# Spreading the softmax's inverse sums through memory, and folding an output projection into the values' weights, in a four-layer image kernel

## The chip, the cores and the metric

The kernel runs on one core of one Trainium2 chip. The metric is the device time of one execution in microseconds; the three timed runs before the change gave 4995.19, 4997.74 and 5000.49 us, so the median is 4997.74 us. The profile is of one execution of the same program. Everything is computed in 32-bit floating point.

## The reference, cut to what matters

The input is a batch of two images of 128 channels and 64 by 64 pixels (4096 pixels). Four layers follow one another:

- layer 0: an embedding, then two state-space ("mamba") blocks with feed-forward parts, run along the 4096 pixels, and a residual
- layer 1: spatial self-attention with 3x3 convolutions for queries, keys and values, and a 1x1 output projection
- layer 2: spatial self-attention with plain projections
- layer 3: convolutions at four scales, a small attention across the scales, normalisation and a fusing projection

The change concerns layers 1 and 2:

```python
# layer 1
q, k, v = conv3x3(x, Wq, bq), conv3x3(x, Wk, bk), conv3x3(x, Wv, bv)    # each 128 x 4096
attn = softmax(einsum('bci,bcj->bij', q, k) * 128**-0.5, axis=2)       # 4096 x 4096
out  = einsum('bij,bcj->bci', attn, v)
x    = x + conv1x1(out, Wo, bo)
# layer 2
attn = softmax(einsum('nci,ncj->nij', q, k), axis=-1)                   # 4096 x 4096
x    = gamma * einsum('ncj,nij->nci', v, attn) + x
```

## The kernel before, in words

The whole program is one `tile_conv_seq`. The images stay in one buffer `xt` on the chip from the first layer to the last. The order of the instructions on each engine is written out by hand: the schedule is manual, so each engine and each issuing queue runs its instructions in the order in which the Python code records them, and waits where a buffer or a value is not ready.

**Layer 0.** Each image has 8 chunks of 512 pixels, and each chunk passes two blocks, which makes 32 items. An item has 32 slots; in each slot one scan runs on VectorE (`scan`, line 411), and the function `background(i)` hangs the other work of neighbouring items on numbered slots of item `i`: embedding, normalisation, projections, gates. Item -1 (`i == -1`) is the lead-in, in which no scan runs yet. There the first chunk goes through its whole chain, and slots 1, 7 and 8 to 10 load and prepare weights: `load_rest` (line 178) loads the 3x3 weights of layer 1 into three tiles `raw`; `fold(which)` (lines 197 to 206) turns each, ten VectorE instructions for each of queries, keys and values, into weights for a fast convolution along the width; `fold_out` (line 210), in slot 23, writes these to `ufold` in memory. Later in the same lead-in come the first `dtb` copies (line 382), the first `times_b` (line 393) and then the scans.

**Layers 1 and 2.** There are four runs: two layers times two images. A run takes its 4096 queries in 16 groups of 256, and each group has 8 units, so there are 512 units in all. A unit `now` consists of:

- `score` (line 759): for 128 queries, the scores against 1024 keys on TensorE; VectorE copies them out of the accumulators and takes maxima (line 764)
- `product` (line 809), 14 units later (`LAG`): for the group's 256 queries, four of the 32 steps of the product of the transposed exponentials `pt` with the values `vt`, into an accumulator `po`

Around them, every four units make a block of 128 queries: `exponentials` (line 774, ScalarE), and twice `turn`: VectorE transposes 32x32 blocks into `tr` (line 789, two buffers), and the blocks are then moved to their partitions in `pt` by four copies on GpSimd (line 796), four transfers issued by ScalarE (line 798) and eight issued by SyncE (line 800). `turn` also computes the inverse sums `rec` of the block, one value for each query, with the queries along the partitions.

The product has the queries along its columns, so each group must turn its 256 inverse sums from a column into a row that stands on all 128 partitions. In the kernel before that is done on the engines: `diagonals` (line 814) multiplies the identity by the inverse sums into two 128x128 tiles `dg` on VectorE, `spread` (line 820) multiplies each by a matrix of ones on TensorE into `pr`, and ScalarE copies that to `rb` (line 822). `divide` (line 834) then multiplies `po` by `rb` into `on`. In layer 1 `finish_mm` (line 841) multiplies `on` by the output projection into an accumulator, two units later, and `finish` (line 845) adds bias and residual into `xt`; in layer 2 `divide` itself adds `gamma` times the result (line 836).

Each transfer signals its end on one of eight semaphores, taken in turn by the transfers of SyncE and ScalarE together, and as built a transfer also waits for the one before it on its semaphore, which is the one eight transfers earlier.

Of the kernel before, what the change touches and what calls it, by code (L numbers as in the profile page):

```python
# [6 lines left out]
F32 = mybir.dt.float32  # L7
AF = mybir.ActivationFunctionType
ALU = mybir.AluOpType
# [6 lines left out]
P = 128  # L16
# [51 lines left out]
def tile_conv_seq(ctx: ExitStack, tc, x, consts, vecs, wemb, wlay, wconv, wdt, wqkv, wsmall, wms, out):  # L68
# [27 lines left out]
    ufold = [ud.tile([P, 18, C], F32, name=f"ufold{k}") for k in range(3)]  # L96

    dkept = [ud.tile([P, 6, 18 * 16], F32, name=f"dkept{k}") for k in range(4)]

    ident = kc[:, K_ID : K_ID + P]  # L100
    cm = kc[:, K_CM : K_CM + P]
# [2 lines left out]
    def v1(name, i=0):  # L104
        return vec[:, VEC[name] + i : VEC[name] + i + 1]
# [10 lines left out]
    with tc.manual_schedule(), ExitStack() as s:  # L116
# [8 lines left out]

        we = wp.tile([P, 2, C], F32, name="we")
        nc.sync.dma_start(we, wemb)


        sel = wp.tile([P, 32], F32, name="sel")  # L130
# [42 lines left out]
        raws, folded = [], []  # L173

        def load_rest():
            for which in range(3):
                raw = sp.tile([P, 3, 3, C], F32, name="raw", tag="h", bufs=5)
                nc.sync.dma_start(raw.rearrange("p y x c -> p (y x) c"), wqkv[:, which])
                raws.append(raw)
            for c in range(NCH):  # L180
                load_x(1, c)
# [4 lines left out]
        for c in range(2, NCH):  # L186
            load_x(0, c)
        load_layer(1)

        def fold(which):  # L190

# [301 lines left out]
        def background(i):  # L493

            todo = [[] for _ in range(NSL)]

            def at(t, f, *a):
                todo[t].append((f, a))

            n, p, q, r = i + 1, i - 1, i - 2, i + 2  # L500
            if has(q):
                at(3, gelu, q)
                at(6, ffn_down, q, (0, 1)), at(7, ffn_down, q, (2, 3)), at(9, ffn_add, q)
                at(11, out_mm, q), at(12, out_add, q)
            if has(p):
                at(7, y_out, p, 1), at(7, gate, p)
                at(9, mix_out, p), at(11, mix_add, p)
            if has(n):
                at(0, pu_taps, n, 0, (0, 1)), at(1, pu_taps, n, 0, (2, 3)), at(2, pu_out, n, 0)
                at(3, pu_taps, n, 1, (0, 1)), at(4, pu_taps, n, 1, (2, 3)), at(5, pu_out, n, 1)  # L510
                at(13, xproj, n), at(14, xproj_out, n), at(14, spread_bc, n, 0), at(22, spread_bc, n, 1)
                at(15, dtproj, n, 0), at(16, dtproj, n, 1), at(17, soft_plus, n), at(18, dt_end, n)
            if has(i):
                at(1, pz_mm, i, 0), at(3, pz_out, i, 0)
                at(5, pz_mm, i, 1), at(6, pz_out, i, 1)
            if has(i) or has(n):
                at(11, silu, i, n)
            if i == -1:
                at(1, load_rest), at(7, prepare, 1)
                for k in range(3):  # L520
                    at(8 + k, fold, k), at(23, fold_out, k)
                at(19, spread_dtu, 0), at(26, times_b, 0)
            pair = [(k, second) for k, second in ((p, True), (r, False)) if has(k)]
            if has(r):
                at(10, embed, r), at(11, embed_out, r)
            w, m = {}, len(pair)
            for k, (it, second) in enumerate(pair):
                at(12 + 2 * k, ln_centre, w, k, it)
                at(13 + 2 * k, ln_square, w, k, it)
                at(27, ln_spread, w, k, m), at(28, ln_scale, w, k, it)  # L530
                at(29, ln_shift, w, k, it, second)
            if pair:
                at(17, ln_var, w, m), at(18, ln_eps, w, m), at(19, ln_rs, w, m), at(20, ln_newton, w, m), at(21, ln_step, w, m)
            if has(p):
                for f in range(4):
                    at(30 + f // 2, ffn_up, p, f)
            if has(i):
                at(24, y_out, i, 0)
            return todo
# [56 lines left out]
            nc.scalar.activation(dst, src, AF.Identity, bias=bias)  # L596

        def bias(r, which):
            return v1("b" + "qkv"[which] + "12"[runs[r][0]])


# [206 lines left out]
                rhs = sta["pt", r, grp, jt // NTH][:, :, jt % NTH, :]  # L808
                nc.tensor.matmul(sta["po", r, grp], lhsT=sta["vt"][:, jt, :], rhs=rhs, start=(jt == 0), stop=(jt == N // P - 1))  # L809

        def diagonals(r, grp):
            for it in range(2):
                dg = sta["dg", it] = sp.tile([P, P], F32, name="dg", tag="dg", bufs=2)
                nc.vector.tensor_scalar(dg, ident, sta["rec", r, grp][:, it : it + 1], None, ALU.mult)

        def spread(r, grp):

            pr = psm.tile([P, QG], F32, name="pr", tag="m")
            for it in range(2):
                nc.tensor.matmul(pr[:, it * P : (it + 1) * P], lhsT=ones, rhs=sta["dg", it], start=True, stop=True)  # L820
            rb = sta["rb", r, grp] = sp.tile([P, QG], F32, name="rb", tag="rb", bufs=2)
            nc.scalar.copy(rb, pr)

        def xg(r, grp):
            l, b = runs[r]
            if l:
                k = QG // W
                return xt[:, b, 1 + grp * k : 1 + (grp + 1) * k, 1 : W + 1]
            cc, i = divmod(grp, 4)
            return xt[:, b, 1 + 16 * cc : 17 + 16 * cc, 1 + i : W + 1 : 4]  # L830

        def divide(r, grp):
            on = sta["on", r, grp] = sp.tile([P, QG], F32, name="on", tag="on")
            nc.vector.tensor_tensor(on, sta.pop(("po", r, grp)), sta.pop(("rb", r, grp)), ALU.mult)
            if runs[r][0]:
                nc.vector.scalar_tensor_tensor(xg(r, grp), rows(on), v1("gamma"), xg(r, grp), ALU.mult, ALU.add)

        def finish_mm(r, grp):
            if not runs[r][0]:
                sta["p2", r, grp] = psm.tile([P, QG], F32, name="p2", tag="m")  # L840
                nc.tensor.matmul(sta["p2", r, grp], lhsT=wa[:, WS_O : WS_O + C], rhs=sta["on", r, grp], start=True, stop=True)

        def finish(r, grp):
            if not runs[r][0]:
                nc.vector.scalar_tensor_tensor(xg(r, grp), sta.pop(("p2", r, grp)).rearrange("p (h w) -> p h w", w=16), v1("bo1"), xg(r, grp), ALU.add, ALU.add)

        def in_turn(f, u0):

# [51 lines left out]
        layers.close()  # L900
        sp = s.enter_context(tc.tile_pool(name="ats", bufs=1, reuse_waits="tile"))
        psa = s.enter_context(tc.tile_pool(name="atpa", bufs=2, reuse_waits="tile", space=PSUM))
        psm = s.enter_context(tc.tile_pool(name="atpm", bufs=1, reuse_waits="tile", space=PSUM))
        for now in range(NALL + LAG + 10):
            r, u = divmod(now, NU)
            w = now % 8
            if now < NALL:
# [42 lines left out]
                elif u == LAG:  # L950
                    load(0, LO), load(0, HI)
                    if r == 0:
                        load(1, LO)
            if w == 7:
                in_turn(lambda r, u: finish_mm(r, u // 8), LAG + 9)
            in_turn(product, LAG)
            if w == 7:
                in_turn(lambda r, u: finish(r, u // 8), LAG + 9)
            if w in (3, 7):
                in_turn(lambda r, u: exponentials(r, u // 4), 3)  # L960
            if w in (1, 5):
# [1 line left out]
            if w in (3, 7):  # L963
                in_turn(lambda r, u: turn(r, u // 4, 1), 7)
            if w == 2:
                in_turn(lambda r, u: diagonals(r, u // 8), 10)
            if w == 3:
                in_turn(lambda r, u: spread(r, u // 8), 11)
            if w == 5:
                in_turn(lambda r, u: divide(r, u // 8), LAG + 7)  # L970
            if now < NCC:
# [501 lines left out]
```

## Time and profile before

| | |
|---|---|
| time, median of three runs | 4997.74 us |
| profiled execution: span from first to last instruction | 4994.0 us |
| median of the runs less that span | 3.7 us |
| TensorE busy | 4661.7 us, 93% of the span |
| VectorE busy | 4022.4 us, 81% |
| ScalarE busy | 2358.4 us, 47% |
| GpSimd busy | 2335.3 us, 47% |
| transfers of `pt` issued by SyncE and by ScalarE | 2048 and 1024, of 64 KB, 2.0 and 2.2 us to landing |

The profiled execution has no separate time; its span stands 3.7 us below the median of the runs. In the profile PE is TensorE's matmul, PEld its weight load, DVE VectorE, ACT ScalarE, POOL GpSimd and SP SyncE; SPq and ACTq are transfers that these two issue. A line such as `L809 PE MATMUL po<-pt,vt` names the line of the kernel, the engine, the output and the inputs. One 32-bit matmul of the program stands as two records. Layer 0 takes the first 2060 us or so, the two attentions last until about 4218 us, and layer 3 takes the rest.

### The profile page before, as it was taken

What the parts mean: (1) busy time and instruction counts of PE and PEld (TensorE: products, weight loads), DVE (VectorE), ACT (ScalarE), POOL (GpSimd) and SP (SyncE); (2) the same over time, 40 slices, a digit from 0 to 9 for tenths busy, and PEclk for the clock granted to TensorE, in tenths of its full rate; (3) what the DMA queues carried; (4) which work ended last, traced back from release to release, by engine and by line L of the source; (5) the groups of instructions that cost most, each with busy time, mean ns of one, the idle gap of its engine ahead of it and who ended that gap; (6) DMA issues with size and microseconds to landing.
All of it is one profiled execution on the core that took longest, in us unless ns stands there. A gap on an engine that the chain in (4) does not pass through costs nothing.

```text
span 4994.0 us, 48951 instructions
## 1 busy us (share of the span) xinstructions
PE 4661.7 (93%) x14797; PEld 2242.2 (45%) x14797; DVE 4022.4 (81%) x4283; ACT 2358.4 (47%) x3218; POOL 2335.3 (47%) x1974
## 2 busy tenths in 40 slices
PE   6898899899988899899999999999999999999997
PEld 2222222222222222366667766666666666333332
DVE  7999999999999999778886677767776775667776
ACT  4677777777777777532222222233233332323332
POOL 3777777666777777513332233323333332333331
PEclk7889998998999989899999999999999999999998
DMA  6233333332333333224444344434444443000000
GB/s 165 68 69 69 69 71 73 71 69 65 67 67 69 69 70 68 71 57 110 109 109 126 105 111 113 118 97 111 113 98 98 110 114 87 3 7 7 5 7 9
DMA packets 242343, 386.24 MB, mean 77 GB/s; under 512 B 88592, under 2 KB 88992, under 8 KB 233632
## 3 DMA queue, kind: packets, MB, share of 16 engines
q1 hardware_dynamic: 192928, 315.94, 26.1%
q10 hardware_dynamic: 49152, 67.17, 5.4%
q8 instruction: 118, 1.93, 0.2%
q14 instruction: 145, 1.19, 0.1%
HBM read 101.02 MB, written 13.37 MB: 23 GB/s over the span
## 4 chain that ended last, share of the span: by engine, by line
PE 46%; POOL 24%; issue 12%; DVE 9%; DMA 3%; SPq 2%; ACT 2%; ACTq 0%; DVEq 0%; POOLq 0%
POOL h L414 19%; PE po L809 13%; PE pq L759 13%; DVE tr L789 3%; DMA pt<-tr 3%; PE pa L656 2%; PE pf L1130 2%; SPq L800 2%; PE pqkv L1157 2%; PE pw L1216 1%; POOL dtu L374 1%; POOL z L437 1%; PE pb L656 1%; PE pfus L1281 1%; PE psc L1181 1%
## 5 line engine op out<-in xcount | busy, mean ns | idle before, releaser
L796 POOL COPY pt<-tr 32x512 f32<-32x512 f32 x1024 | 648.8, 634 | 1439.2 <-DVE tr L789 704.5
L411 DVE TENSOR_TENSOR_SCAN h<-da,carry,h 128x512 f32<-128x512 f32 x1024 | 1240.7, 1265 | 62.0 <-ACT da L400 31.8
L414 POOL TENSOR_TENSOR h<-h,cb 128x2048 f32<-128x2048 f32 x256 | 1160.8, 4535 | 20.7
L759 PE MATMUL pq<-k,q 128*128 128x512 f32 x2048 | 962.6, 593 | 6.9 <-DVE sc L764 6.9
L809 PE MATMUL po<-pt,vt 128*128 128x256 f32 x4096 | 965.6, 379 | 2.5 <-DMA pt<-tr 2.5
L774 ACT ACTIVATE sc<-sc,nm 128x2048 f32<-128x2048 f32 x256 | 510.5, 1995 | 914.9 <-DVE nm L770 685.8
L809 PEld LDWEIGHTS po<-pt,vt 128*128 128x128 f32 x4096 | 777.9, 190 | 294.8 <-issue 208.3
L764 DVE TENSOR_SCALAR_CACHE_REDUCE sc<-pq 128x1024 f32<-128x1024 f32 x512 | 624.7, 1221 | 315.4 <-PE pq L759 293.8
L400 ACT ACTIVATE da<-dtb,am 128x512 f32<-128x512 f32 x1024 | 681.4, 684 | 220.9 <-DVE h L411 207.6
L789 DVE STREAM_TRANSPOSE tr<-sc 128x2048 f32<-128x2048 f32 x256 | 591.6, 2311 | 65.6 <-DMA pt<-tr 56.3
L393 DVE TENSOR_TENSOR h<-bb,pdu 128x2048 f32<-128x2048 f32 x256 | 581.3, 2271 | 77.6 <-PE py L426 29.4
L426 PE MATMUL py<-h,sel 128*32 128x512 f32 x2048 | 510.8, 642 | 1.6 <-POOL h L414 1.6
L759 PEld LDWEIGHTS pq<-k,q 128*128 128x128 f32 x2048 | 382.9, 190 | 283.0 <-issue 247.2
L387 PE MATMUL pdu<-dtu,fsel 128*128 128x512 f32 x512 | 327.6, 726 | 103.0 <-DVE h L393 100.6
L426 PEld LDWEIGHTS py<-h,sel 128*32 128x32 f32 x2048 | 115.3, 118 | 415.9 <-issue 409.0
L314 PE MATMUL pu<-xn,wu 128*128 128x512 f32 x512 | 246.4, 615 | 7.2 <-ACT u L320 5.5
L387 PEld LDWEIGHTS pdu<-dtu,fsel 128*128 128x128 f32 x512 | 96.6, 215 | 310.2 <-DVE h L393 185.9
L413 POOL COPY carry<-h 128x4 f32<-128x4 f32 x256 | 47.7, 186 | 389.8 <-DVE h L411 389.8
L1223 DVE TENSOR_TENSOR ov<-v,pw 128x2048 f32<-128x2048 f32 x64 | 146.1, 2284 | 62.1 <-PE pw L1216 62.1
L1157 PE MATMUL pqkv<-f,ws 128*128 128x512 f32 x384 | 188.1, 615 | 3.0 <-DVE prod L1174 2.3
L1227 POOL TENSOR_TENSOR ov<-ov 128x2048 f32<-128x2048 f32 x16 | 72.5, 4534 | 235.7 <-DVE ov L1223 235.7
L374 POOL TENSOR_TENSOR dtu<-dt,u 128x1024 f32<-128x1024 f32 x32 | 75.2, 2350 | 188.7 <-ACT dt L368 188.7
(259 smaller groups left out, 5262.2 us busy)
## 6 DMA issues: line engine op xcount, KB each, us to landing
pt<-tr SPq DMA_DIRECT2D x2048, 64.0 KB, 2.0
dtb<-dt SPq DMA_DIRECT2D x1024, 64.0 KB, 2.0
pt<-tr ACTq DMA_DIRECT2D x1024, 64.0 KB, 2.2
bb<-dr SPq DMA_DIRECT2D x128, 256.0 KB, 4.4
cb<-dr SPq DMA_DIRECT2D x128, 256.0 KB, 4.7
uw<-ufold SPq DMA_DIRECT2D x12, 576.0 KB, 4.9
uw<-dkept SPq DMA_DIRECT2D x20, 288.0 KB, 3.1
xt<-in_x SPq DMA_DIRECT2D x16, 256.0 KB, 4.8
```

The lines of the kernel that those rows point to most:

```text
L387: nc.tensor.matmul(pdu, lhsT=four(s_ % 4), rhs=st[i]["dtu"][:, s_ // 4, :], start=True, stop=True)
L393: nc.vector.tensor_tensor(h, st[i]["bc", 0], pdu.unsqueeze(1).to_broadcast([P, 4, CH]), ALU.mult)
L400: nc.scalar.activation(da, st[i]["dtb", s_], AF.Exp, scale=am[items[i][1]][:, j, gg, m : m + 1])
L411: nc.vector.tensor_tensor_scan(h[:, m, :], da, h[:, m, :], carries[b, l][:, j, gg, m : m + 1], ALU.mult, ALU.add)
L414: nc.gpsimd.tensor_tensor(h, h, st[i]["bc", 1], ALU.mult)
L426: nc.tensor.matmul(py[r : r + 32, :], lhsT=sel, rhs=st[i]["h", s_ + k][:, m, :], start=(m == 0), stop=(m == 3), tile_position=(0, r),)
L759: nc.tensor.matmul(pq[:, i, :], lhsT=sta["q", r, grp][:, it * P : (it + 1) * P], rhs=sta["k"][:, at : at + CH], start=True, stop=True)
L764: nc.vector.tensor_scalar(dst, pq, 1.0, None, ALU.mult, ALU.max, accum_out=sta["mx"][:, c2 : c2 + 1])
L774: nc.scalar.activation(sc, sc, AF.Exp, bias=nm, scale=scale, accum_out=sm[:, hh : hh + 1])
L789: nc.vector.transpose(tr, sta.pop(("sc", r, blk, hh)).rearrange("p (t r f) -> p r t f", r=NB, f=32))
L796: nc.gpsimd.tensor_copy(dst, src)
L809: nc.tensor.matmul(sta["po", r, grp], lhsT=sta["vt"][:, jt, :], rhs=rhs, start=(jt == 0), stop=(jt == N // P - 1))
```

## The change

The inverse sums go through memory. Two small tensors `sums`, of 2 by 128 values, are added in memory. `sums_out` writes the 256 inverse sums of a group there from `rec` (128 partitions, two values each, that stand 128 values apart in memory), and `sums_in`, two units later, reads the 256 values back to every one of 128 partitions as `rb`. Both are issued by SyncE. `diagonals`, `spread`, the accumulators `pr` and their ScalarE copy are gone.

The output projection of layer 1 is folded into the weights of its values. `through_out`, recorded in slot 9 of the lead-in item, transposes the nine 128x128 weight matrices of the values in `raw[2]`, multiplies each by the projection `wo`, and puts the products back in `raw[2]`, before `fold(2)` works on it in slot 10. It also multiplies the values' bias (`bvo`). `wo` is loaded ahead of the three `raw` tiles. `finish_mm` and its accumulator are gone, `divide` multiplies `po` in place, and in both layers the addition to `xt` follows directly in `divide`.

```diff
+    sums = [ud.tile([2, P], F32, name=f"sums{k}") for k in range(2)]
...
+        wo = wp.tile([P, C], F32, name="wo")
+        bvo = kp.tile([P, 1], F32, name="bvo")
...
         def load_rest():
+            nc.sync.dma_start(wo, wsmall[:, WS_O : WS_O + C])
             for which in range(3):
...
+        def through_out():
+
+            raw = raws[2].rearrange("p y x c -> p (y x) c")
+            for turn in (True, False):
+                for k in range(0, 9, 3):
+                    pv = mm.tile([P, 3, C], F32, name="pv", tag="mm")
+                    for i in range(3):
+                        if turn:
+                            nc.tensor.transpose(pv[:, i, :], raw[:, k + i, :], ident)
+                        else:
+                            nc.tensor.matmul(pv[:, i, :], lhsT=raw[:, k + i, :], rhs=wo, start=True, stop=True)
+                    nc.scalar.copy(raw[:, k : k + 3, :], pv)
+            pb = mm.tile([P, 1], F32, name="pbv", tag="mm")
+            nc.tensor.matmul(pb, lhsT=wo, rhs=v1("bv1"), start=True, stop=True)
+            nc.scalar.copy(bvo, pb)
...
-                at(1, load_rest), at(7, prepare, 1)
+                at(1, load_rest), at(7, prepare, 1), at(9, through_out)
...
         def bias(r, which):
+            if which == 2 and not runs[r][0]:
+                return bvo
             return v1("b" + "qkv"[which] + "12"[runs[r][0]])
...
-        def diagonals(r, grp):
-            for it in range(2):
-                dg = sta["dg", it] = sp.tile([P, P], F32, name="dg", tag="dg", bufs=2)
-                nc.vector.tensor_scalar(dg, ident, sta["rec", r, grp][:, it : it + 1], None, ALU.mult)
-
-        def spread(r, grp):
-
-            pr = psm.tile([P, QG], F32, name="pr", tag="m")
-            for it in range(2):
-                nc.tensor.matmul(pr[:, it * P : (it + 1) * P], lhsT=ones, rhs=sta["dg", it], start=True, stop=True)
+        def sums_out(r, grp):
+            nc.sync.dma_start(sums[grp % 2].rearrange("i p -> p i"), sta.pop(("rec", r, grp)))
+
+        def sums_in(r, grp):
             rb = sta["rb", r, grp] = sp.tile([P, QG], F32, name="rb", tag="rb", bufs=2)
-            nc.scalar.copy(rb, pr)
+            src = sums[grp % 2].rearrange("(o i) p -> o (i p)", o=1)
+            nc.sync.dma_start(rb, src.to_broadcast([P, QG]))
...
         def divide(r, grp):
-            on = sta["on", r, grp] = sp.tile([P, QG], F32, name="on", tag="on")
-            nc.vector.tensor_tensor(on, sta.pop(("po", r, grp)), sta.pop(("rb", r, grp)), ALU.mult)
+            po = sta.pop(("po", r, grp))
+            nc.vector.tensor_tensor(po, po, sta.pop(("rb", r, grp)), ALU.mult)
             if runs[r][0]:
-                nc.vector.scalar_tensor_tensor(xg(r, grp), rows(on), v1("gamma"), xg(r, grp), ALU.mult, ALU.add)
-
-        def finish_mm(r, grp):
-            if not runs[r][0]:
-                sta["p2", r, grp] = psm.tile([P, QG], F32, name="p2", tag="m")
-                nc.tensor.matmul(sta["p2", r, grp], lhsT=wa[:, WS_O : WS_O + C], rhs=sta["on", r, grp], start=True, stop=True)
-
-        def finish(r, grp):
-            if not runs[r][0]:
-                nc.vector.scalar_tensor_tensor(xg(r, grp), sta.pop(("p2", r, grp)).rearrange("p (h w) -> p h w", w=16), v1("bo1"), xg(r, grp), ALU.add, ALU.add)
+                nc.vector.scalar_tensor_tensor(xg(r, grp), rows(po), v1("gamma"), xg(r, grp), ALU.mult, ALU.add)
+            else:
+                by = po.rearrange("p (h w) -> p h w", w=16)
+                nc.vector.scalar_tensor_tensor(xg(r, grp), by, v1("bo1"), xg(r, grp), ALU.add, ALU.add)
...
-        psm = s.enter_context(tc.tile_pool(name="atpm", bufs=1, reuse_waits="tile", space=PSUM))
-        for now in range(NALL + LAG + 10):
+        for now in range(NALL + LAG + 8):
...
-            if w == 7:
-                in_turn(lambda r, u: finish_mm(r, u // 8), LAG + 9)
             in_turn(product, LAG)
-            if w == 7:
-                in_turn(lambda r, u: finish(r, u // 8), LAG + 9)
...
             if w == 2:
-                in_turn(lambda r, u: diagonals(r, u // 8), 10)
-            if w == 3:
-                in_turn(lambda r, u: spread(r, u // 8), 11)
+                in_turn(lambda r, u: sums_out(r, u // 8), 10)
+            if w == 4:
+                in_turn(lambda r, u: sums_in(r, u // 8), 12)
             if w == 5:
                 in_turn(lambda r, u: divide(r, u // 8), LAG + 7)
```

## The prediction, made before the changed kernel ran

> **What bounds the kernel now.** I read the busy table by stretches first, to see which engine fills the two attentions (columns: stretch, its length, then busy us of PE, PEld, DVE, ACT, POOL, then granted clock, DMA share, GB/s):
>
> ```profile
> 2700.00:3200.00 500.00, 496.01 (x1851) 344.91 (x1850) 358.51 (x559) 138.23 (x159) 146.72 (x240) 1.00 0.44 111
> 3330.00:4180.00 850.00, 843.36 (x3010) 560.96 (x3009) 636.69 (x932) 269.63 (x304) 286.22 (x464) 0.99 0.44 108
> ```
>
> TensorE is busy 99% of both stretches at full clock, while VectorE is idle a quarter of the time. Busy matmuls are modelled, so I checked with the timeline of PE, by the start of each row:
>
> ```profile
> 2860.80 1.88 PE L759 MATMUL pq<-k,q 128*128 128x512 f32 x4
> 2862.52 0.59 PE L841 MATMUL p<-on,wa 128*128 128x256 f32 x2
> 2862.95 1.89 PE L809 MATMUL po<-pt,vt 128*128 128x256 f32 x8
> ...
> 2876.72 1.89 PE L809 MATMUL po<-pt,vt 128*128 128x256 f32 x8
> 2878.45 0.61 PE L820 MATMUL pr<-dg,kc 128*128 128x128 f32 x4
> 2878.89 1.88 PE L759 MATMUL pq<-k,q 128*128 128x512 f32 x4
> ```
>
> Scores start to product 1.72 us, product to the next scores 1.72: a unit is 3.44 us of back-to-back matmuls. Line 841 pushes the product back by 0.43 us, line 820 the next scores by 0.44. So in the attentions TensorE's issue order is the path. Third, TensorE's waits from 2195 to 2700 us, the first run (columns: us in total, times, longest), where VectorE also makes convolution inputs and is busy 81% (93% from 2200 to 2250):
>
> ```profile
> PE pq L759 <- DVE sc L764: 6.9, 10, 2.0
> PE p L841 <- DVE on L834: 3.5, 7, 0.8
> PE pr L820 <- DVE dg L814: 1.8, 1, 1.8
> ```
>
> Last, the timeline of the lead-in, where `through_out` goes:
>
> ```profile
> 34.81 1.28 ACT L334 ACT_TABLE_LOAD   x1
> ...
> 38.88 0.69 ACT L243 ACTIVATE xt<-pe,vec 128x512 f32<-128x512 f32 x1 [0.41 <-PE pe L239]
> ...
> 41.62 3.63 PE L343 MATMUL pd<-u,wl 128*40 128x512 f32 x4
> ...
> 58.35 2.29 DVE L393 TENSOR_TENSOR h<-bb,pdu 128x2048 f32<-128x2048 f32 x1
> 59.33 24.24 SPq L382 DMA_DIRECT2D dtb<-dt  x24
> 60.55 0.74 DVE L291 SCALAR_TENSOR_TENSOR cen<-cen,vec,pr 128x512 f32<-128x512 f32 x1
> 61.21 4.80 DVE L411 TENSOR_TENSOR_SCAN h<-da,carry,h 128x512 f32<-128x512 f32 x4
> ...
> 69.89 1.91 ACT L400 ACTIVATE da<-dtb,am 128x512 f32<-128x512 f32 x3 [6.65 <-DMA dtb<-dt]
> ```
>
> Before the first scan nothing is throughput: it is one chain of single steps, and a step put into it moves the rest.
>
> **The change part by part.** Removed `spread`: 64 groups x 0.44 us = 28.2. In the last group TensorE afterwards waits 2.52 us for `pt` transfers anyway, so I count 63: **-27.7** (at most 64 x the row's modelled 0.61 = 39.0; at least 26).
>
> Removed `finish_mm`: 32 groups of layer 1 x 0.43 = **-13.8** (19.6 by the busy time of its group; no less, the starts being measured).
>
> TensorE's waits on VectorE for those two matmuls (3.5 and 1.8) go, and VectorE loses two `dg` of 0.42 us per group. But its groups also become 0.87 us shorter, so its lag, which showed at `p`, may next show at `sc` (6.9 now). Taken **-3.5**; bounds 0 and -12.2, the three rows together.
>
> Off the path: 128 `dg` (53.5 us of VectorE, 460 ns each as recorded), 64 copies `rb` on ScalarE (373 ns): 0, TensorE being the cover; in the first run, where VectorE is near the bound, that gain is inside the -3.5.
>
> `divide` in place: no row has VectorE writing an accumulator. Nearest are `on` (accumulator in, 386 ns) and `xt<-p` (676 ns). Taken 386, at worst 676, which is 0.3 us per group against VectorE's 142 idle us of 500, or 8 us per group: 0, and up to +1 in the first run. The accumulator `po` is held one instruction longer, and its buffer is wanted again 9 units (31 us) later: 0. The residual's addition in layer 1 moves two units earlier on VectorE; same work.
>
> `sums_out` and `sums_in` on SyncE:
>
> ```profile
> L800 SPq DMA_DIRECT2D pt<-tr x1424: 507/589/1967, 2711.7 to 4097.3; - x178
> SPq L800 <- DVE tr L789: 417.0, 173, 17.6
> xt<-in_x SPq DMA_DIRECT2D x16, 256.0 KB, 4.8
> ```
>
> An issue holds SyncE 0.59 us (min/median/max in the first line). A `tr` comes every 6.88 us, and its eight issues take 4.7; SyncE waits 417/173 = 2.4 us for each next `tr`. One more issue between two turns fits in that, with 1.8 over. `sums_out` stands behind a turn whose `tr` came after `rec`, so it waits for nothing. `sums_in` waits on SyncE until `sums_out` has landed, but it stands behind the next turn's eight copies, and the fourth of those already waits for `sums_out`, being eight transfers later. From the issue of `sums_out` that is about 6.9 + 2.3 + 3 x 0.59 - 7.0 = 4 us away (a turn, its transpose, three issues, less the previous turn's end). What lies behind: the rest of that turn's `pt`, then through `tr`'s two buffers VectorE's transpose two turns on (another 4.8 us of slack: 13.8 less 2.3, 4.7 and 2.0 to land), and TensorE, which uses these `pt` seven units (24 us) later. So a landing up to about 8.8 us costs nothing. Nearest rows: `xt<-in_x` moves 1024 pieces of 256 bytes in 4.8 us, and `dr<-dbl` (chip to memory, 64 KB) lands after 1.6. `sums_out` has 256 pieces of 4 bytes; I take 3 us, ends 1.6 and 4.8: 0. `rb` is wanted 9 units after `sums_in`: 0. ScalarE's and GpSimd's queues get no new transfer. At the very end of layer 2 nothing hides the two issues: `sums_out` stands before the last turn's copies, which the last product waits for: +0.6; with the wait of the last group **+1** (0 to 3).
>
> The Trainium skill speaks against this transfer ("DMA: Bandwidth & Descriptors", section "Rules for kernel authors"): a non-contiguous last dimension becomes one descriptor per element, and its "Specifications" say that transfers under 512 bytes are read, modified and written. It gives no time for that; if it doubled the 4.8 us row (an estimate), 9.6 us would pass 8.8 by 0.8, and 64 x 0.8 = 51 us would make the sum 5013 instead of 4962. No run before shows such a transfer.
>
> `through_out`, in the lead-in. TensorE: 9 transposes and 18 records of 128 columns, 0.11 us each at full clock (0.44 for four) and twice that at the 0.50 granted from 40 to 45 us: 3.0 to 5.9 us. ScalarE: 6 copies of 384 columns, between 0.373 (256) and 0.587 (512), so 0.48 each: 2.9. They alternate over two accumulators with a hand-over each way of some 0.2 us, so six rounds of about 1.2 to 1.6 us from 37.7 on: ScalarE ends near 44 to 45. Its next work, the table load of `silu` (34.81 before), comes 8.5 to 10 us later, and with it `xt<-pe` (38.88), which the matmuls `pc` and then `pd` (41.62) wait for. The raw weights (issued by 20.7, landing in 9.3) are there; `wo` adds a 64 KB transfer before them: 0. What hides some: VectorE's folds end at 58.3, and `pdu` was ready at 53.3, so `times_b` moves only about 4. But `cen` (60.55) waited for a matmul that ended at 58.45, 2 us of slack, so the first scan moves 6.5 to 8. And SyncE's order puts `dr`, `bb`, `dtb`, `cb`, `fold_out` behind each other, so the second group's `dtb`, issued at 59.33 and waited for until 69.89, moves by all 8 to 9. From there VectorE works almost without gaps and the shift stays: **+8** (+4 if the clock is full and `pd`, at half speed in its 3.63 us, gets quicker; +11 if the rounds do not overlap).
>
> Sum: -27.7 - 13.8 - 3.5 + 1 + 8 = -36.0. The span of 4994.0 becomes 4958.0; with the 3.7 by which the median stands above the span, **4961.7 us**. With all terms at their ends: -26 - 13.8 + 1 + 3 + 11 = -25 (4973), and -39 - 19.6 - 12.2 + 0 + 4 = -67, which I cut to -50 (4948) because the starts, not the modelled durations, carry the first two.
>
> A second rule: "Perfetto Trace Analysis", section "Identifying the Most-Contended Engine", calls matmul busy time a bad measure and prefers that of weight loads. By that measure (344.9 of 500, 69%) TensorE has room, and 0.69 of 41.5 would give 4975 instead of 4962. The starts show no room.
>
> **The rivals.** *TensorE's freed time is taken by VectorE in the first run.* For: VectorE 81 to 93% busy there, TensorE already waiting on `sc`. Against: VectorE loses as much per group as TensorE. Price: 16 groups x 0.87 = 13.9 and the 3.5 not gained: 4979.
>
> *The lead-in hides `through_out`.* For: the folds on VectorE end late, at 58.3. Against: `cen` and the `dtb` transfers do not wait for the folds alone. Price: 8 back: 4954.
>
> *The way through memory stalls SyncE: slower.* One mechanism: `sums_out` lands after 8.8 us, the turn behind it is late, VectorE waits for `tr`'s buffer, TensorE for scores. Each us beyond costs 64 us; it decides from 8.8 + 36/64 = 9.4 us on. At 10 us: 4962 + 64 x 1.2 = 5039. For: pieces of 4 bytes, of which no row tells. Against: 1024 pieces of 256 bytes take 4.8.
>
> *The change doesn't do what it says*: the matmuls leave, but TensorE's order was not the path and only +8 + 1 - 3.5 stay: 5003. Against: the starts above.
>
> **How the numbers follow.** Forecast with its own range of 4948 to 4973: 0.67. First-run rival 0.11, hidden lead-in 0.10, SyncE 0.07, no effect 0.05. The range 4946 to 4984 takes in the first three and leaves out the last two and some spread. A measurement of this kernel can tell about 0.2%, 10 us. Faster (under 4988) holds the forecast and both neighbours, less 0.02 for an overrun of the first: 0.86; slower 0.07 and half of the no-effect case: 0.10; same 0.04.
>
> **What would show it.** Right: scores follow the product 1.72 us later in every unit and a group of clean units takes 27.5 us (28.4 now) in layer 1; the first scan starts near 68 us and the second group's `da` near 78; `sums` lands within 5 us; SyncE still waits for `tr`, about 1.8 us per turn. Wrong: new waits of `tr` on transfers, `po` on `pt`, or `divide` on `rb`; a `divide` far above 0.4 us; a lead-in that moves by 15 us or not at all.

## The result, and the profile after

The changed kernel takes 5036.42 us (median of 4 runs, 5031.53 to 5038.76), against 4996.63 us for the kernel before on the same chip. The ratio is 1.0078 with a 95% interval from 1.0064 to 1.0093: slower by 40 us, where the prediction had 36 us faster. The span of the profiled execution went from 4994.0 to 5034.9 us.

Where the 40.9 us of span lie is read from three starts: the first record of `pq` (scores), the last of `po` (product), and the end. Until the first `pq`, before needed 2184.7 us and after 2194.4: +9.7. From there to the last `po`, the two attentions, 2032.8 became 2061.5: +28.7, where the prediction's terms add up to -44.0. The rest is +2.5. So the lead-in behaved about as foreseen, and the attentions lost what they should have gained and 29 us more.

The same two stretches as were shown of before, from the table by stretches (stretch, length, then busy us of PE, PEld, DVE, ACT, POOL, granted clock, DMA share, GB/s):

```profile
2700.00:3200.00 500.00, 476.60 (x1736) 329.24 (x1735) 335.34 (x513) 126.02 (x140) 135.99 (x224) 0.98 0.43 111
3330.00:4180.00 850.00, 833.45 (x2908) 548.81 (x2907) 603.28 (x871) 258.86 (x282) 276.84 (x456) 0.99 0.45 110
```

TensorE was busy 496.01 of the first 500 us and is now busy 476.60. Nothing has become busier: every engine does less in the stretch. The time has become waiting. Over the attentions as a whole, TensorE is busy 1997.1 of 2032.8 us in before and 1969.1 of 2061.5 in after, so it idles 92.4 us instead of 35.7. Who waits is seen in the waits of the two attentions, 2100 to 4260 us (us in total, times, longest), of after:

```profile
ACT sc L796 <- DMA pt<-tr: 673.2, 63, 15.7
...
DVE tr L811 <- DMA pt<-tr: 174.8, 184, 6.9
...
PE pq L781 <- DVE sc L786: 34.8, 35, 3.6
```

In before the same three stood at 229.0, 56.3 and 6.9 us. The first two wait for the copies `pt<-tr`, the transfers that the change does not touch; how the third follows from them is shown on one group below. The third is 28 us of the 57 us of new idle time of TensorE; the rest stands in waits between the runs and before single products, and is not followed here. SyncE's waits, 2300 to 4200 us, of after:

```profile
SPq L822 <- DMA pt<-tr: 237.4, 74, 7.4
SPq L822 <- DVE tr L811: 164.5, 44, 16.0
SPq L822 <- DMA rb<-sums: 44.8, 54, 1.4
SPq L822 <- DMA sums<-rec: 36.9, 6, 8.1
```

In before SyncE waited 548.0 us for `tr`, 223 times, which is the wait of a queue that is ahead of its work, and 9.1 us for copies. Now it is late: it waits for transfers that have not landed. The new write itself, and the copies on SyncE's queue from 2300 to 4200 us (instructions with their issue time in ns as min/median/max, and under each the us from issue to landing):

```profile
L834 SPq DMA_DIRECT2D sums<-rec x64: 578/582/707, 2229.2 to 4237.0; - x64
...
DMA to landing us min/median/max: 7.4/8.4/10.5
...
L822 SPq DMA_DIRECT2D pt<-tr x1897: 507/589/3742, 2300.0 to 4199.8; - x190
...
DMA to landing us min/median/max: 1.9/2.0/10.4
```

One kilobyte takes 8.4 us to land. The copies keep their median of 2.0 us, but the slowest takes 10.4 (4.8 in before): as long as the write. One group on three queues shows how that reaches TensorE; it is the one in which the write took longest, 10.5 us. SyncE first, after, 2955 to 2992 us (start, us, engine, line, output from input, how many):

```profile
2960.52 0.58 SPq L834 DMA_DIRECT2D sums<-rec  x1
2961.20 12.90 SPq L822 DMA_DIRECT2D pt<-tr  x8
2974.15 0.58 SPq L839 DMA_DIRECT2D rb<-sums  x1
```

Eight copies need 4.7 us in before; here they need 12.90. Three are issued by 2962.97, and then none until 2971.05, as the same view cut to 2968 to 2976 us shows:

```profile
2971.05 3.05 SPq L822 DMA_DIRECT2D pt<-tr  x5
```

In the same stretch ScalarE with its own queue, then VectorE, then TensorE, each from its timeline (in brackets the idle time before it and what ended it):

```profile
2959.35 15.47 ACTq L820 DMA_DIRECT2D pt<-tr  x7
2974.92 2.00 ACT L796 ACTIVATE sc<-sc,nm 128x2048 f32<-128x2048 f32 x1 [15.66 <-DMA pt<-tr]
```

```profile
2975.71 2.31 DVE L811 STREAM_TRANSPOSE tr<-sc 128x2048 f32<-128x2048 f32 x1 [6.86 <-DMA pt<-tr]
```

```profile
2973.93 1.89 PE L831 MATMUL po<-pt,vt 128*128 128x256 f32 x8
2979.44 1.98 PE L781 MATMUL pq<-k,q 128*128 128x512 f32 x4 [3.62 <-DVE sc L786]
```

SyncE's gap, 8.1 us, is the wait of the fourth copy for the write itself (`SPq L822 <- DMA sums<-rec: 8.1, 1, 8.1` among SyncE's waits of this stretch). But the copies that were issued ahead of the gap land no earlier: SyncE's first two behind the write, issued at 2961.2 and 2961.8, after 10.4 and 10.0 us, and ScalarE's two, issued at 2960.6 and 2961.9, after 10.6 and 10.0. That is 2971.2 to 2972.0, just behind the write at 2971.0. They do not lack room to move their bytes, as the table by stretches (columns as above) shows for the time between:

```profile
2964.20:2972.00 7.80, 7.80 (x30) 5.34 (x30) 4.06 (x9) 0.00 (x0) 2.43 (x4) 1.00 0.00 0
```

The DMA share is 0.00: no transfer moves anything, and what is outstanding is the landing of the write and of the copies behind it.

The copies on both queues stand still, the exponentials on ScalarE (line 796) stand behind ScalarE's copies, VectorE's next transpose (line 811) waits for copies, its score reduction `sc` stands behind that transpose, and TensorE waits 3.62 us for it. Where no such wait stands, the product follows the scores and the scores the product after 1.72 us, as foreseen.

### The profile page after: what moved, and what is told of

Same layout as the page of the kernel before. It is cut to its first block, busy times and chain, and to the rows that moved or that the text cites. A ratio compares the mean times of both kernels' runs of the same rounds, so it can differ in the third digit from the quotient of the medians.

```text
span 5034.9 us, 48294 instructions
## 1 busy us (share of the span) xinstructions
PE 4641.8 (92%) x14506; PEld 2211.2 (44%) x14506; DVE 3970.9 (79%) x4155; ACT 2335.6 (46%) x3161; POOL 2328.9 (46%) x1974
## 4 chain that ended last, share of the span: by engine, by line
PE 33%; POOL 22%; DMA 12%; issue 12%; DVE 10%; SPq 7%; ACT 3%; ACTq 0%; DVEq 0%; POOLq 0%
POOL h L434 18%; DMA pt<-tr 8%; PE pq L781 7%; SPq L822 7%; PE po L831 6%; DVE tr L811 3%; PE pf L1136 2%; PE pqkv L1163 2%; DVE sc L786 2%; PE pa L678 2%; DMA rb<-sums 2%; DMA sums<-rec 2%; PE py L446 1%; PE pw L1222 1%; POOL dtu L394 1%
## 5 line engine op out<-in xcount | busy, mean ns | idle before, releaser
L796 ACT ACTIVATE sc<-sc,nm 128x2048 f32<-128x2048 f32 x256 | 510.4, 1995 | 1007.9 <-DMA pt<-tr 673.2
```

Of the source, the lines that this page charges most:

```text
L796: nc.scalar.activation(sc, sc, AF.Exp, bias=nm, scale=scale, accum_out=sm[:, hh : hh + 1])
```

## The experiments

Theory W, from the profile after: the write of the inverse sums lands late, holds the copies behind it, and alone costs what the attentions lost. Rivals: R1, the folding or the division in the accumulator costs it; R2, the read back or SyncE's two more issues cost it; R3, under W, the price is that of 256 small pieces as such, or that of how they lie in memory. "Attentions" is the time from the first `pq` to the last `po` of the profiled run (before: 2032.8).

"Not recorded" means that the trace of that run holds no landings of the write.

| kernel | median us | before beside it | ratio, 95% interval | attentions | write lands after |
|---|---|---|---|---|---|
| after | 5036.42 | 4996.63 | 1.0078 (1.0064 to 1.0093) | 2061.5 | 8.4 |
| fold_only | 4993.30 | 4995.92 | 0.9994 (0.9984 to 1.0003) | 2013.4 | no write |
| sums_only | 5030.58 | 4996.69 | 1.0072 (1.0058 to 1.0086) | 2068.3 | not recorded |
| no_write | 4969.66 | 4995.92 | 0.9951 (0.9937 to 0.9966) | 1995.7 | no write |
| turned | 4969.40 | 4995.92 | 0.9949 (0.9934 to 0.9963) | 1992.6 | not recorded |
| late_read | 5023.39 | 4995.92 | 1.0058 (1.0043 to 1.0073) | 2048.0 | 8.3 |
| pool_write | 4998.81 | 4996.69 | 1.0008 (0.9999 to 1.0018) | 2023.0 | 8.3 |
| eight_bytes | 4965.41 | 4996.69 | 0.9939 (0.9926 to 0.9953) | 1992.5 | 3.3 |
| far_apart | 4971.22 | 4995.35 | 0.9949 (0.9934 to 0.9964) | 1995.5 | 2.0 |
| one_column | 5009.47 | 4995.35 | 1.0028 (1.0017 to 1.0039) | 2029.9 | 8.1 |
| turned_early | 4963.53 | 4996.69 | 0.9936 (0.9923 to 0.9948) | 1995.4 | not recorded |
| eight_early | 4957.58 | 4995.35 | 0.9926 (0.9913 to 0.9938) | 1992.2 | 3.3 |

### Which half of the change: fold_only and sums_only

fold_only is the changed kernel with the engines' way of spreading put back:

```diff
...
-            if w == 2:
-                in_turn(lambda r, u: sums_out(r, u // 8), 10)
-            if w == 4:
-                in_turn(lambda r, u: sums_in(r, u // 8), 12)
+            if w == 2:
+                in_turn(lambda r, u: diagonals(r, u // 8), 10)
+            if w == 3:
+                in_turn(lambda r, u: spread(r, u // 8), 11)
```

> The changed kernel with the inverse sums spread by VectorE, TensorE and ScalarE as before; the projection stays folded into the values' weights and divide stays in place. Theory (the element-wise write of the sums, landing after 8.4 us, is the whole loss): the projection's matmuls are gone (-13.8 us, and some of their waits), the lead-in costs its +8, so about 4990 us, and the attention of the profile is about 14 us shorter than before. Rival (divide in place or the folding itself costs the time): 5015 us or more.

sums_only is the other half, the kernel before with `sums_out` and `sums_in` of the change, `finish_mm` and `on` kept:

```diff
...
-            if w == 2:
-                in_turn(lambda r, u: diagonals(r, u // 8), 10)
-            if w == 3:
-                in_turn(lambda r, u: spread(r, u // 8), 11)
+            if w == 2:
+                in_turn(lambda r, u: sums_out(r, u // 8), 10)
+            if w == 4:
+                in_turn(lambda r, u: sums_in(r, u // 8), 12)
```

> The kernel before with the inverse sums spread through memory as in the change, everything else as before: the projection stays a matmul per group, divide writes to a buffer of its own, and nothing is added in the lead-in. Theory (the write is the whole loss, and the folding alone gave about -3): 5035 to 5045 us. Rival (it needs divide in place or the folding as well to lose): 5000 us or less.

The folding alone gives 4993.30 us, no measurable change: its attentions are 19.4 us shorter, and its first `pq` starts 10.9 us later. The spread through memory alone gives 5030.58, nearly all of the loss (a little less than the 5035 to 5045 expected), without any division in the accumulator. R1 is out.

### The write taken away: no_write

```diff
-            nc.sync.dma_start(sums[grp % 2].rearrange("i p -> p i"), sta.pop(("rec", r, grp)))
+            rec = sta.pop(("rec", r, grp))
+            if r == 0 and grp < 2:
+                nc.sync.dma_start(sums[grp % 2].rearrange("i p -> p i"), rec)
```

> The changed kernel with the write of the sums issued only for the first two groups of the first run; the reads into all partitions stay as they are, every group. Left out: the inverse sums of all later groups, which are divided by those of the first two. Theory (the write's landing holds back the transfers behind it): 4960 to 4970 us, and SyncE waits for VectorE's transposes again. Rival (the read of 128 KB, or more issues on SyncE): half of the loss or more stays, 5005 to 5036 us. Rival (divide in place): 5036 us.

With the read and its issue left in place, 4969.66 us, and 65.8 us less in the attentions than after. R2 is out: reading 256 values back to 128 partitions for every group, and its issue on SyncE, cost nothing that shows.

### The same values in rows: turned

A 32x32 transpose on VectorE puts the sums in rows, and two writes of four pieces of 128 bytes take the place of the 256 pieces. `recw`, two buffers of 32 columns, takes the place of `rec`; the sums stand in its first two columns:

```diff
...
-            nc.sync.dma_start(sums[grp % 2].rearrange("i p -> p i"), sta.pop(("rec", r, grp)))
+            rt = sp.tile([P, 32], F32, name="rt", tag="rt", bufs=2)
+            nc.vector.transpose(rt, recw[grp % 2])
+            for it in range(2):
+                dst = sums[grp % 2][it : it + 1, :].rearrange("o (b f) -> (o b) f", f=32)
+                nc.sync.dma_start(dst, rt[it : it + 97 : 32, :])
...
```

> The changed kernel with the inverse sums turned by one 32x32-block transpose on VectorE per group, and written in two transfers of four pieces of 128 bytes each instead of 256 pieces of 4 bytes; three issues a group on SyncE instead of two. Theory: the two writes land in 2 to 3 us, nothing behind them is held, and the time is 4962 to 4972 us. Rival (issues on SyncE): 5040 us or more, there being more of them.

4969.40 us: one more VectorE instruction and one more issue on SyncE in each group, and the kernel is as fast as without a write. SyncE's waits, 2300 to 4200 us, are again those of a queue that is ahead:

```profile
SPq L820 <- DVE tr L809: 357.5, 192, 15.7
...
SPq L820 <- DMA pt<-tr: 16.4, 21, 2.5
```

### The queue: late_read and pool_write

late_read issues `sums_in` four units later (in w 0, offset 16), so that the read finds the write landed; copies can still wait for the write, through the semaphores. pool_write does that too, and has GpSimd issue the write:

```diff
-            if w == 4:
-                in_turn(lambda r, u: sums_in(r, u // 8), 12)
+            if w == 0:
+                in_turn(lambda r, u: sums_in(r, u // 8), 16)
...
-            nc.sync.dma_start(sums[grp % 2].rearrange("i p -> p i"), sta.pop(("rec", r, grp)))
+            nc.gpsimd.dma_start(sums[grp % 2].rearrange("i p -> p i"), sta.pop(("rec", r, grp)))
```

> The changed kernel with the read of the sums recorded four units later (six units after the write instead of two), so that it finds the write landed. Theory (the copies behind the write wait for it, by their semaphores and in the same rings): little changes, 5020 to 5040 us. Rival (SyncE stands at the read until the write has landed): the loss goes, 4962 to 4980 us.

> The changed kernel with the element-wise write of the sums issued by GpSimd, so that it takes neither SyncE's ring nor one of the eight semaphores that SyncE's and ScalarE's transfers share; the read stays on SyncE, recorded four units later. The write is the same 256 pieces of 4 bytes. Theory (SyncE's copies stand behind the write, in its ring and by its semaphore): 4968 to 4985 us though the write still lands after 7 us or more. Rival (the pieces hold the transfer engines themselves, whoever issues them): 5005 us or more.

late_read gives back only 13 us. pool_write, at 4998.81, fell between the two expectations: its attentions are 38.5 us shorter than those of after and still 30.5 longer than with a fast write (2023.0 against 1992.5 in eight_bytes). The write and the copies in pool_write:

```profile
L834 POOL DMA_DIRECT2D sums<-rec x64: 723/723/929, 2225.4 to 4191.0; - x64
...
DMA to landing us min/median/max: 7.4/8.3/9.7
...
L822 SPq DMA_DIRECT2D pt<-tr x1953: 507/589/3170, 2301.4 to 4199.6; - x196
...
DMA to landing us min/median/max: 1.9/2.1/9.6
```

The landing of the write does not depend on the queue that issues it, and copies still land as late as 9.6 us although the write is no longer in their queue. So what stands in SyncE's queue, the read's place included, is a good half of the loss (38.5 of 69.0 us), and the rest remains without it. Part of what holds the copies there is seen in a single write of pool_write, with one copy of SyncE and one of ScalarE that were issued after it:

```profile
L834 POOL DMA_DIRECT2D sums<-rec x1: 723/723/723, 2727.5 to 2727.5; - x1
...
DMA to landing us min/median/max: 8.1/8.1/8.1
```

```profile
L822 SPq DMA_DIRECT2D pt<-tr x1: 590/590/590, 2729.6 to 2729.6; - x1
...
DMA to landing us min/median/max: 6.4/6.4/6.4
```

```profile
L820 ACTq DMA_DIRECT2D pt<-tr x1: 517/517/517, 2732.0 to 2732.0; - x1
...
DMA to landing us min/median/max: 4.7/4.7/4.7
```

Issued 2 and 4 us after the write and on two other queues, both land within about 1 us behind it. It is so throughout this trace: of the 280 copies with a recorded landing that SyncE and ScalarE issued after a write and more than 2.2 us before that write landed, none landed ahead of it. And since each transfer waits for the one eight earlier on its semaphore, copies that land late hold the next ones back on both queues. How much of the 30.5 us this makes, and how much GpSimd's own issues of the write (0.72 us each), was not measured apart.

### Fewer and longer pieces: eight_bytes

The two values of a partition lie next to each other in memory, so the write has 128 pieces of 8 bytes, and `divide` reads `rb` with step 2:

```diff
-    sums = [ud.tile([2, P], F32, name=f"sums{k}") for k in range(2)]
+    sums = [ud.tile([P, 2], F32, name=f"sums{k}") for k in range(2)]
...
-            nc.sync.dma_start(sums[grp % 2].rearrange("i p -> p i"), sta.pop(("rec", r, grp)))
+            nc.sync.dma_start(sums[grp % 2], sta.pop(("rec", r, grp)))
...
-            nc.vector.tensor_tensor(po, po, sta.pop(("rb", r, grp)), ALU.mult)
+            by2 = po.rearrange("p (i q) -> p i q", i=2)
+            nc.vector.tensor_tensor(by2, by2, sta.pop(("rb", r, grp)).rearrange("p (q i) -> p i q", i=2), ALU.mult)
```

> The changed kernel with the sums in memory in the order in which they stand on the chip, so that the write has 128 pieces of 8 bytes instead of 256 of 4; divide reads rb with a step of two. Theory (the landing goes by the number of pieces): the write lands after about 5 us, and 4975 to 5005 us. Rival (the landing is a fixed cost of such a write): 8.4 us and 5030 us or more.

The expectation was wrong to the good side: half the pieces land in 3.3 us, not 5, and 4965.41 us is all of the gain. The write, SyncE's waits from 2300 to 4200 us, and TensorE's clean stretch, of eight_bytes:

```profile
L834 SPq DMA_DIRECT2D sums<-rec x64: 572/580/1220, 2230.1 to 4169.9; - x64
...
DMA to landing us min/median/max: 2.9/3.3/4.6
```

```profile
SPq L822 <- DVE tr L811: 411.9, 207, 15.7
...
SPq L822 <- DMA pt<-tr: 16.9, 18, 2.5
```

```profile
2700.00:3200.00 500.00, 495.76 (x1805) 340.87 (x1804) 358.74 (x539) 136.79 (x148) 150.55 (x248) 1.00 0.46 117
```

That the landing fell by more than half suggested that the number of pieces alone is not the price. Two runs separate number, size and place.

### Number, size or place: far_apart and one_column

Both write the sums, from the third group on, to a scratch area that is never read, so both leave out the later groups' sums from the division, as no_write does. far_apart keeps 256 pieces of 4 bytes and puts them 64 bytes apart; one_column keeps them side by side and writes half of them:

```diff
+    far = [ud.tile([P, 2, 16], F32, name=f"far{k}") for k in range(2)]
...
+                nc.sync.dma_start(far[grp % 2][:, :, 0], rec)
```

```diff
+    far = [ud.tile([1, P], F32, name=f"far{k}") for k in range(2)]
...
+                nc.sync.dma_start(far[grp % 2].rearrange("o p -> p o"), rec[:, 0:1])
```

> As the kernel after, but from the third group on the write of the inverse sums goes, as 256 pieces of 4 bytes, to a scratch area in memory that no one reads, where neighbouring pieces lie 64 bytes apart instead of 4 (no_write's division by the first two groups' sums is kept, so the spread values are left out of the computation). Theory A, the time lies in the 4-byte pieces themselves (their number, or a price of each): the landing stays near 8.4 us, SyncE's copies stay held and the time is 5025 to 5040 us. Theory B, the time lies in neighbouring pieces meeting in one line of memory (16 pieces to 64 bytes in the kernel after, 8 in the eight-byte form): the landing falls to 3.5 us or less and the time to 4965 to 4975 us.

> As far_apart, but only one of the group's two columns is written: 128 pieces of 4 bytes that lie next to each other in memory (512 bytes in all); read and division as in no_write, so the spread values are left out of the computation. If the price is by the number of pieces with any size, the landing is that of the 128 eight-byte pieces, 3.3 us, and the time 4965 to 4975 us. If it is a price of the 4-byte piece, the landing is half of 8.4 us, 4.2 us, or more; at 4.2 us the time is still below 4985 us, at 6 us or more above 4990 us.

The writes of far_apart, and then those of one_column:

```profile
L839 SPq DMA_DIRECT2D far<-rec x62: 582/592/1586, 2286.5 to 4172.4; - x62
...
DMA to landing us min/median/max: 1.9/2.0/2.9
```

```profile
L839 SPq DMA_DIRECT2D far<-rec x62: 570/581/1177, 2286.7 to 4206.1; - x62
...
DMA to landing us min/median/max: 6.7/8.1/9.6
```

256 pieces of 4 bytes land in 2.0 us when they lie 64 bytes apart, and 128 of them need 8.1 when they lie side by side. So for the landing, neither the number of pieces nor their size by itself is the price: it is that pieces of one write are neighbours. With 16 pieces to 64 bytes it is 8.1 to 8.4 us, with 8 (eight_bytes) 3.3, with one 2.0. Whether the pieces of eight_bytes land sooner because fewer of them share a stretch or because each is longer, where between 4 and 64 bytes the distance stops to matter, and what in the memory makes it so, was not tried. Nor does the landing alone set the loss: one_column lands as late as late_read (8.1 and 8.3 us), and like there no read waits for the write, yet its attentions are 18.1 us shorter (2029.9 and 2048.0). Why, these runs do not tell.

### The lead-in: turned_early and eight_early

`wo` and `raw[2]` are loaded right behind layer 0's weights, and the rounds of `through_out` are moved one item earlier, to slots 19 and 21 of item -2 (`through` is one round, `through_bias` the bias):

```diff
         load_layer(0)
+        nc.sync.dma_start(wo, wsmall[:, WS_O : WS_O + C])
+        nc.sync.dma_start(raws[2].rearrange("p y x c -> p (y x) c"), wqkv[:, 2])
...
-                at(1, load_rest), at(7, prepare, 1), at(9, through_out)
+                at(1, load_rest), at(7, prepare, 1)
...
+            if i == -2:
+                at(19, through, True, 0), at(19, through, True, 3)
+                at(21, through, True, 6)
+                for k in range(0, 9, 3):
+                    at(21, through, False, k)
+                at(21, through_bias)
```

> The kernel that turns the inverse sums on VectorE before writing them, with the values' weights and the projection loaded right after the first layer's weights and the folding spread over the gaps of the first normalisation (item -2, slots 19 and 21), so that nothing of it stands in the first chunk's chain. Theory (the lead-in cost 8 to 11 us because ScalarE's copies stood before silu): the first scan comes at 61 to 64 us as before, and the time is 8 to 11 us below the turned version: 4958 to 4962 us. Rival (the shift is made up later, or the early loads delay the first chunk as much): 4966 to 4975 us.

> turned_early's lead-in (output weights and values' weights loaded right behind layer 0's, the folding's 18 products moved two items of work earlier) with the eight-byte write in place of the turn. The parts were measured apart: eight-byte write 4965.4 us, the earlier lead-in 5.9 us less than turned (4963.5 against 4969.4). If they add, 4958 to 4961 us; if the eight-byte form already hides part of the lead-in's lag, 4962 to 4966 us.

turned_early takes 5.9 us off turned; its first `pq` starts at 2189.2 us instead of 2196.5. By time alone that is not sure, as the runs of the two overlap (4956.74 to 4967.37 and 4966.87 to 4971.23), and 4963.53 lies between what the expectation and its rival gave. With the eight-byte write the two gains add, and there the runs lie apart: 4957.58 us (4956.38 to 4961.19) against 4965.41 (4963.94 to 4965.79), 0.9926 of before (0.9913 to 0.9938), the fastest version here. Its first scans, from VectorE's timeline of eight_early:

```profile
63.00 4.80 DVE L431 TENSOR_TENSOR_SCAN h<-da,carry,h 128x512 f32<-128x512 f32 x4
...
73.05 4.81 DVE L431 TENSOR_TENSOR_SCAN h<-da,carry,h 128x512 f32<-128x512 f32 x4 [3.06 <-ACT da L420]
```

They start 1.8 and 2.4 us later than in before (61.21 and 70.62), instead of 5.2 and 8.1 in after.

## Why the prediction was wrong

The step that failed is the term of the write, put at nothing: "`sums_out` has 256 pieces of 4 bytes; I take 3 us, ends 1.6 and 4.8: 0". The write measured 8.4 us, outside both ends, and cost 69.0 us of the attentions (2061.5 against 1992.5 in eight_bytes), 1.08 us a group. Two things in it were wrong, the landing and what a landing costs. For the landing, both rows behind the ends were rows of other shapes: `xt<-in_x` has 1024 pieces of 256 bytes, and what had to be priced was neighbouring pieces far smaller than that. A row in which the pieces are 64 times as long says nothing about neighbours within one short stretch of memory, and the range should have stayed open above.

The cost is the failure that decided, in "a landing up to about 8.8 us costs nothing". 8.4 is below 8.8, so with the right landing the prediction would still have forecast a gain. Nor is it the late writes alone: of the 46 whose landing is recorded, 12 passed 8.8 us, by 4.9 us together, which at the sum's price is some 7 us for 64 (an estimate). The sum let only the fourth copy behind the write wait. The trace shows two things beside that: the copies that are issued while the write is under way land late themselves (10.4 us at most), so that SyncE waits mostly for copies (237.4 us) and little for the write (36.9); and ScalarE's queue, which "get[s] no new transfer", is held as well (its copies land after up to 10.6 us, 4.8 in before), and with it the exponentials that stand behind its copies. Their waits grew from 229.0 to 673.2 us; eight_bytes, which loses nothing, has 385.3 of them. pool_write, with the write out of SyncE's queue and 30.5 us still lost, shows that more than that queue's order is at work.

So the rival that came true is *the way through memory stalls SyncE*, given 0.07, and in a harsher form than it was put: its threshold of 9.4 us for a slower kernel was too high. That its price for a landing of 10 us, 5039, comes near the measured 5036 is luck: the landing was 8.4, for which the same rule gives no loss. The rest of the prediction can be read off eight_bytes, the same change with a write that lands early: 4965.41 us, where 4961.7 was forecast.

- *Attentions.* The terms made -44.0 (-27.7, -13.8, -3.5, +1); eight_bytes shows -40.3. The split was off: fold_only shows -19.4 for the folding, more than the 13.8 and all of the 3.5, and what is left for the spread is -20.9, not -27.7; each of these is one profiled execution, and the runs of fold_only spread over 12.8 us. TensorE's waits for VectorE did not vanish: `p` and `pr` waited 5.3 us in the first run, both are gone, but in their place the scores wait 14.4 us for `sc` instead of 6.9. Against -3.5 that is +2.2, the shift that the prediction named and did not count. The other us of the spread are not accounted for.
- *Weight loads as the measure.* The second rule, that TensorE has room because weight loads fill only 69%, would have made 4975 of it; the measured 4965.41 lies between that and the sum by starts, and nearer to the starts.
- *Division in the accumulator.* Taken 386 ns, at worst 676. Right, in after:

```profile
L851 DVE TENSOR_TENSOR po<-po,rb 128x256 f32<-128x256 f32 x64 | 25.7, 401 | 20.0 <-PE po L831 20.0
```

- *The lead-in.* Taken +8 (4 to 11), with the first scan near 68 and the second group's `da` near 78. After has the first scan at 66.42 and, in ScalarE's timeline:

```profile
77.98 1.91 ACT L420 ACTIVATE da<-dtb,am 128x512 f32<-128x512 f32 x3 [9.53 <-DMA dtb<-dt]
```

  That is +8.1 (69.89 in before). The first scan moved by 5.2, less than the 6.5 to 8 taken. ScalarE's next work behind the rounds came 8.9 us later, within the 8.5 to 10 taken:

```profile
43.68 1.28 ACT L354 ACT_TABLE_LOAD   x1
```

  But the working does not give that: six rounds of 1.2 to 1.6 us from 37.7 on end at 44.9 to 47.3, not at 44 to 45; the rounds took about 1 us. Until the first `pq` the shift has become +9.7, and over the runs with this lead-in it is +9.3 (far_apart) to +11.8 (turned), at the upper end of the range and past it.

The Trainium skill's rule that was weighed against the change, "DMA: Bandwidth & Descriptors", "Rules for kernel authors" (a non-contiguous last dimension becomes one descriptor per element), is borne out: on the first DMA queue far_apart has 125388 packets from 2300 to 4200 us and eight_bytes 117474, 130 more for each of 61 writes that have 128 pieces more. That page's "Specifications", by which transfers under 512 bytes are read, modified and written, does not price it: pieces of 4 bytes landed in 2.0 us as well as in 8.4. That neighbours in one stretch wait for each other's reading and writing would fit both, but it is argued and not shown.

## What to carry to other kernels

Before values go through memory, look at how the pieces of the write lie there: a column of single values written side by side is the slow form, and storing each partition's values together, turning them first, or leaving gaps brought the whole loss back at a cost too small to see (with gaps, the write alone was tried; the values were not read back). Price a small transfer by the transfers around it, not by its bytes: here it cost the delay of the copies that were issued while it was under way, on its own queue and on others, and every engine that issues copies passes that on to the work behind them. And a small preparation put into a chain without slack costs its whole length; done one item earlier, the same work moved the first scan by 1.8 us instead of 5.2.

## What was not expected of the hardware

A write of 1 KB as 256 neighbouring pieces of 4 bytes needs 8.4 us to land and one of half as many 8.1, while the same 256 pieces 64 bytes apart need 2.0, as little as a 64 KB copy of `pt`. The late write delays transfers of another engine's queue, though no transfer moves anything meanwhile (DMA share 0.00 from 2964.2 to 2972.0 us): ScalarE's copies landed after up to 10.6 us beside it, and after at most 4.6 in eight_bytes. In pool_write, where the write has a queue of its own, none of the 280 copies issued behind it landed ahead of it. And VectorE multiplies in place in the accumulator in 401 ns, against 386 ns into another buffer in before.
